# A fused convolution block on one core: the squeeze-and-excite step moved to VectorE, set-up work moved off VectorE, and the seam between the first two stages rebuilt

## The chip, the cores and the metric

The program runs on one core of a Trainium2 chip. The time is the device time of one execution in microseconds. A run gives three executions, and the median of them is the time of the kernel. One further execution was profiled; its instructions are what the views below show.

## The reference, cut to what matters

The input `x` has 16 images of 192 channels and 64x64 pixels, in float32. Two layers follow each other.

```python
# layer 0
h = ln2d(x)                                   # normalise over the 192 channels
projected, gate = split(conv1x1(h, in_proj))  # 192 -> 384
projected = dwconv3(projected, dw_k)
mixed = (four_directional_scans(projected) + dwconv3(projected, le_k)) * sigmoid(gate)
mixed = gelu(batch_norm(mixed))               # statistics over all 16 images
x = x + conv1x1(mixed, out_proj)
x = x + conv1x1(gelu(conv1x1(ln2d(x), fc1)), fc2)   # 192 -> 768 -> 192
# layer 1
pooled = x.mean(axis=(2, 3))                  # one number per image and channel
t = relu(gamma * (pooled @ w1.T - running_mean) * rsqrt(running_var + eps) + beta)   # squeeze, 48 numbers
wt = (t @ w2.T + b2) * mask                   # excite: four 3x3 taps per image and channel are left
out = depthwise_conv(x, wt) + bias
```

## The kernel before, in words

**First stage (0 to 591 us).** The loop `for n in range(n_ac)` runs over 64 chunks of 512 columns, of two images (a pair) each, one in each half of the partitions. For each chunk `turn` (L486, tiles `ps_xt`) transposes pixels on TensorE, `variance` (L493, L494) takes their statistics on VectorE, `project` multiplies by the weights `wi` (L515, tiles `ps_pj`), and the products leave PSUM on VectorE (L520) and ScalarE (L521), into `stg` and `mid` in turn, four chunks to a block. `store` (L539) writes the blocks to DRAM scratch `pg_d`, in five parts by channel group, and `store_first` (L533) sends the first channel group to the tile `low` by DMA. The input tile `xa` has four buffers; `load_a` (L473) asks for it three chunks ahead, half on SyncE's queue and half on GpSimd's.

Work that only sets up the later stages is put between the chunks: `beside(n, f)` in the list `side` calls `f` after chunk `n`. `gate_bias`, `decay_rows`, `projection_bias`, `tap_sums`, `columns`, `sums_across` and `conv_bias` make per-channel biases with small matmuls and small VectorE operations. `vector`, `runs` and `store_vector` build the vectors from which the convolution matrices `dm` and `lm` are read back by `load_dm` (L193) and `load_lm` (L201). `load_weights(k)` loads weights: `k == 1` is the 1.18 MB of `wf1`.

**Second stage (592 to 1265 us).** 96 steps, each with two groups of 64x64 matmuls: `depthwise` (L630, `ps_d`), which uses `dm`, and `local` with `vertical` (L674, `ps_l`), which use `lm`. ScalarE copies `ps_d` into `q` and makes the decay tables `tab` (L653). VectorE runs two scans (L665, L667), the gate (L708) and statistics (L710). A channel group of eight takes four steps; `load_pg` (L617) brings the next group back from DRAM. The seam between the first two stages starts with `hidden_bias` (L141): 36 matmuls with one moving column, put where the first group is on its way to `low`.

**Seam to the third stage (1260 to 1290 us).** `spread` and `batch_norm` turn the statistics into scales through TensorE and VectorE, `keep_up(k)` (L759) issues `k` matmuls that nobody reads, and the first chunk runs without overlap.

**Third stage (1290 to 3557 us).** The loop `for n in range(n_ch + 1)` runs over 64 chunks, eight to a pair. A chunk is one sequence of matmuls: `first` (L997), means and variances, `out_proj` for chunk `n + 2`, and the seven products of `second` (`both`, L852). When a pair has ended (`ended is not None`), `pooled` (L1110) adds up its sums, `squeeze` (L1116) and `excite` (L852, `ps_k`) make the four taps per channel, and `dynamic` spreads the depthwise convolution (L65 and ScalarE) over the next chunks. After the last pair `dynamic_last` runs alone. The order on every engine is the order in which the program is written.

The lines that the steps of the prediction rest on:

```python
for n in range(n_ac):
    if n + 3 < n_ac: load_a(n + 3)
    ...                      # stores of the block before
    project(n, ...); turn(n + 1); deviation(n + 1)
    for f, args in side.pop(n, ()): f(*args)
```

Of the kernel before, what the change touches and what calls it, by code (L numbers as in the profile page):

```python
# [55 lines left out]
def conv_block_kernel(ctx: ExitStack, tc: tile.TileContext, x, prm, w_in, w_out, w_fc1, b_fc1, w_fc2, w1, bn1, w2, out):  # L56
# [46 lines left out]
    w2t = k2.tile([RED, NTAP, C], F32, tag="w2t", name="w2t")  # L103
    b1 = k2.tile([RED, 4], F32, tag="b1", name="b1")
    s1 = k2.tile([RED, 1], F32, tag="s1", name="s1")

    mean64 = k2.tile([128, 64], F32, tag="mean64", name="mean64")

    def load_weights(k):
# [10 lines left out]
        elif k == 3:  # L120
            nc.sync.dma_start(bf1, b_fc1)
            load_cls3(w1t, w1)
            nc.sync.dma_start(w2t, w2[:, 0:NTAP, :])
        else:
            nc.sync.dma_start(b1, bn1)
            nc.sync.dma_start(pv[:, 0], prm[0:128])
            for q in HALF:
                nc.sync.dma_start(pv[q, 1], prm[128:C])


    def squeeze_scale():
# [4 lines left out]
        nc.vector.tensor_scalar_mul(w1t, w1t, 1.0 / NPIX)  # L136

# [28 lines left out]
    ones = ce.tile([128, 128], F32, tag="ones", name="ones")  # L166
    pv = ce.tile([128, 2, NPRM], F32, tag="pv", name="pv")
# [11 lines left out]
    mats[0]["lm"] = lm_even  # L179
    mats[1]["lm"] = mid[:, NPG:NPG + 5 * HW * (GC // 2)].rearrange("p (k m c) -> p k m c", k=5, m=HW)  # L180
# [69 lines left out]
    with ExitStack() as stage:  # L250
# [45 lines left out]
        def gate_bias():  # L296
# [5 lines left out]
            nc.vector.tensor_copy(bias_g, pb[:, 0:C])  # L302

        def by_half(dst, src):

            for i, q in enumerate(HALF):
                nc.vector.tensor_copy(dst[q].rearrange("p (g c) -> p g c", c=GC // 2),
                                      src[q].rearrange("p (g i c) -> p g i c", i=2, c=GC // 2)[:, :, i])
# [23 lines left out]
        def tap_sums(t):  # L332
            taps9 = pt3[lo, t, DW:DW + 9].rearrange("p (i j) -> p j i", j=3)
            for k, rr in enumerate((slice(0, 3), slice(1, 3), slice(0, 2))):
                nc.vector.tensor_reduce(sv[:, t, k, 1:3], taps9[:, 0::2, rr], AX.X, ALU.add)
                nc.vector.tensor_reduce(sv[:, t, k, 0:1], taps9[:, 1:2, rr], AX.X, ALU.add)
                nc.vector.tensor_add(sv[:, t, k, 0:1], sv[:, t, k, 0:1], sv[:, t, k, 1:2])
                nc.vector.tensor_add(sv[:, t, k, 0:1], sv[:, t, k, 0:1], sv[:, t, k, 2:3])
            nc.vector.tensor_scalar_mul(sv[:, t], sv[:, t], bp[:, t:t + 1])
            nc.vector.tensor_scalar_mul(sv[:, t, :, 1:3], sv[:, t, :, 1:3], -1.0)  # L340

        def columns():
            pi = bank()
            nc.tensor.transpose(pi[0:3, 0:128], ind, ident)
            nc.vector.tensor_copy(indt, pi[0:3, 0:128])

        def sums_across(k):
# [3 lines left out]
            nc.vector.tensor_copy(svt, pr[0:3, 0:C])  # L351
# [38 lines left out]
        def vector(k):  # L390
            nc.gpsimd.memset(slots[k % 2], 0.0)
            if k < 3:
                nc.vector.tensor_copy(slots[k % 2].rearrange("g (s c) -> g s c", c=GC)[:, 62:65],
                                      ptg[:, :, DW + 3 * k:DW + 3 * k + 3].rearrange("g c j -> g j c"))
                return
            for i in range(2):
                gv, c = slot(k)[:, i], slice(i * (GC // 2), (i + 1) * (GC // 2))
                if k < 6:
                    le = ptg[:, c, LE + 3 * (k - 3):LE + 3 * (k - 3) + 3]
                    nc.vector.tensor_copy(gv[:, 62:65], le[:, :, ::-1].rearrange("g c j -> g j c"))  # L400
                else:
                    nc.vector.tensor_copy(gv[:, 63:64], gaing[:, c, k - 4:k - 3].rearrange("g c j -> g j c"))

        def runs(i, d):

            gv, c = slot(4)[:, i], slice(i * (GC // 2), (i + 1) * (GC // 2))
            nc.vector.memset(imp, 0.0)
            nc.vector.tensor_copy(imp[:, :, 0:1], gaing[:, c, d:d + 1])
            nc.vector.memset(dcol[:, :, 0:1], 0.0)
            nc.vector.tensor_copy(dcol[:, :, 1:HW], decg[:, c, d:d + 1].broadcast_to([NCG, GC // 2, HW - 1]))  # L410
# [3 lines left out]
            nc.vector.tensor_add(vec, vec, run.rearrange("g c m -> g m c"))  # L414
# [26 lines left out]
        for k, n in enumerate((13, 14, 15, 16, 24, 32, 33, 34)):  # L441
            beside(n, vector, k)
            if k == 4:
                for j in range(4):
                    beside(n + 1 + j, runs, j // 2, j % 2)
            beside(n + (5 if k == 4 else 1), store_vector, k)
        for k in (0, 1, 3, 4):
            beside(40 + k, load_weights, k)
        for i in range(2):
            for h in range(2):  # L450
                beside(45 + 8 * i + 2 * h, load_dm, i, (h,))
                beside(49 + 8 * i + 2 * h, load_lm, i, (h,))
# [82 lines left out]

        def store(blk, d, queues):
# [58 lines left out]
        store_first(blk)  # L595
# [3 lines left out]
    with ExitStack() as stage:  # L599
# [168 lines left out]
        for k in range(-2, n_bp + 1):  # L768
            if 0 <= k + 1 < n_bp:
# [15 lines left out]
            if k == -2:  # L785
                hidden_bias(psb.tile([128, 2, CH], F32, tag="l", name="pb_h")[:, 0])
            if k + 2 < n_bp:
                depthwise(k + 2)
            if 0 <= k < n_bp:
                local(k)  # L790
                sigmoid(k)
            if k in (1, 3, 5):
                scale_hidden(k // 2)
            if k == n_bp - hp_:

# [624 lines left out]
```

## Time and profile before

| | |
|---|---|
| Median of three runs | 3562.65 us (3562.14 to 3562.84) |
| Profiled execution, its own time | 3559.31 us |
| Span of the profiled execution | 3557.5 us |
| Busy share of the span | TensorE 99%, weight loads 53%, VectorE 77%, ScalarE 52%, GpSimd 32% |
| Mean granted TensorE clock | 0.995 |
| Chain that ended last, by engine | TensorE 89%, VectorE 1%, DMA 1% |

A busy share says how long an engine had an instruction in flight. TensorE is one queue: a matmul that is not needed at its place still pushes all that follow it. "Granted clock" is the share of the full TensorE clock in a stretch. Idle time in front of an instruction is shown in brackets with what ended it. The profiled execution was 3.3 us shorter than the median of the runs.

### The profile page before, as it was taken

How to read it: one execution, taken by the hardware profiler on the slowest of the kernel's cores; microseconds unless marked ns; L12 is line 12 of the kernel's file. 1: busy time of each engine (PE TensorE's matmuls, PEld its weight loads, DVE VectorE, ACT ScalarE, POOL GpSimd, SP SyncE). 2: the span in 40 equal slices, each digit the busy share in tenths (PEclk: the TensorE clock that was granted, in tenths of full speed). 3: DMA queues.
4: the chain of work that ended last, by engine and by line, in shares of the span. 5: the costliest groups of instructions: out<-in, count | busy, mean ns of one | idle time of the engine just before them, and what ended most of it. 6: DMA issues, size and time to landing. Idle time of an engine off the chain costs nothing.

```text
span 3557.5 us, 79074 instructions
## 1 busy us (share of the span) xinstructions
PE 3525.5 (99%) x33426; PEld 1874.6 (53%) x33426; DVE 2741.6 (77%) x4722; ACT 1834.7 (52%) x2067; POOL 1155.7 (32%) x1246
## 2 busy tenths in 40 slices
PE   9999999999999999999999999999999999999998
PEld 6666866555555544454444444444445444444443
DVE  7888776999999975557777776777677777767765
ACT  3444445888888844344444445454444444453543
POOL 3434342111111134333333333343433333343433
PEclk9999999999999999999999999999999999999999
DMA  7999998999999941112222222222222222232213
GB/s 177 263 272 264 271 294 282 282 301 283 280 282 286 247 123 34 40 54 60 69 71 70 67 65 81 58 75 62 80 60 69 68 74 62 68 82 58 75 34 90
DMA packets 288987, 492.29 MB, mean 138 GB/s; under 512 B 24816, under 2 KB 183016, under 8 KB 288632
## 3 DMA queue, kind: packets, MB, share of 16 engines
q1 hardware_dynamic: 246772, 341.85, 35.8%
q0 software_dynamic: 40928, 144.36, 14.2%
q8 instruction: 263, 4.31, 0.5%
q10 hardware_dynamic: 932, 1.03, 0.1%
q14 instruction: 92, 0.75, 0.1%
HBM read 284.95 MB, written 197.92 MB: 136 GB/s over the span
## 4 chain that ended last, share of the span: by engine, by line
PE 89%; DVE 1%; DMA 1%; issue 0%; ACT 0%; SPq 0%; ACTq 0%; POOL 0%; DVEq 0%
PE ps_f L997 28%; PE ps_f L852 19%; PE ps_l L674 11%; PE ps_pj L515 7%; PE ps_d L630 7%; PE ps_s L852 7%; PE ps_o L907 5%; PE ps_o L900 2%; PE ps_m L936 1%; PE ps_v L936 1%; PE ps_xt L486 1%; PE ps_k L852 0%; DMA pg_d<-mid 0%; DMA xa<-in_x_dram 0%; DMA mixed_d<-mid 0%
## 5 line engine op out<-in xcount | busy, mean ns | idle before, releaser
L997 PE MATMUL ps_f<-h,wf 64*64 64x512 f32 x9216 | 1014.9, 590 | 0.0
L999 ACT ACTIVATE gl<-ps_f,bf 128x1024 f32<-128x1024 f32 x384 | 427.8, 1114 | 1082.3 <-PE ps_f L997 1080.0
L997 PEld LDWEIGHTS ps_f<-h,wf 64*64 64x64 f32 x9216 | 346.2, 133 | 599.0 <-issue 575.1
L852 PE MATMUL ps_f<-gl,place 128*64 128x256 f32 (+1 forms) x3072 | 528.7, 486 | 1.1 <-ACT rs L979 1.1
L515 PE MATMUL ps_pj<-wi,xa 64*128 64x384 f32 x3072 | 520.1, 488 | 9.2 <-DVE stg L520 6.2
L515 PEld LDWEIGHTS ps_pj<-wi,xa 64*128 64x128 f32 x3072 | 334.0, 189 | 159.9 <-DVE stg L520 10.5
L1032 POOL TENSOR_TENSOR gl<-gl 128x512 f32<-128x512 f32 x192 | 308.6, 1634 | 159.2 <-PE ps_f L852 159.0
L852 PEld LDWEIGHTS ps_f<-gl,place 128*64 128x64 f32 x3072 | 225.2, 137 | 217.7 <-issue 145.8
L1022 POOL COPY turn<-o 128x1 f32<-128x1 f32 x84 | 16.4, 195 | 832.8 <-DVE o L65 832.8
L1028 POOL TENSOR_TENSOR t<-gl 128x512 f32<-128x512 f32 x192 | 246.0, 1281 | 89.0 <-ACT gl L999 44.6
L1030 POOL TENSOR_TENSOR t<-gl,t 128x512 f32<-128x512 f32 x192 | 247.0, 1287 | 44.2 <-ACT gl L999 30.8
L65 DVE SCALAR_TENSOR_TENSOR o<-ximg,taps,o 128x1024 f32<-128x1024 f32 x180 | 231.8, 1288 | 4.9
L473 POOL DMA_DIRECT2D xa<-in_x_dram x192 | 120.2, 634 | 323.8 <-PE ps_pj L515 277.1
L665 DVE TENSOR_TENSOR_SCAN v<-tab,q 128x1024 f32<-128x1024 f32 x96 | 218.3, 2274 | 7.8 <-ACT tab L653 7.8
L667 DVE TENSOR_TENSOR_SCAN v<-tab,q 128x1024 f32<-128x1024 f32 x96 | 217.5, 2266 | 0.0
L1055 DVE SCALAR_TENSOR_TENSOR ximg<-ps_f,pt,ximg 128x256 f32<-128x256 f32 (+1 forms) x176 | 96.6, 549 | 151.2 <-PE ps_f L852 151.2
L653 ACT ACTIVATE tab<-mask,dec_b 128x1024 f32<-128x1024 f32 x192 | 209.6, 1144 | 0.0
L521 ACT ACTIVATE mid<-ps_pj,rsa 128x384 f32<-128x384 f32 x128 | 119.5, 937 | 167.0 <-PE ps_pj L515 150.1
L521 ACT ACTIVATE stg<-ps_pj,rsa 128x384 f32<-128x384 f32 x128 | 119.2, 935 | 162.6 <-PE ps_pj L515 144.2
L913 DVE SCALAR_TENSOR_TENSOR ximg<-ps_o,pt,low 128x256 f32<-128x256 f32 x264 | 113.0, 478 | 93.0 <-PE ps_o L907 90.3
L907 PE MATMUL ps_o<-low,wo 128*64 128x256 f32 x1536 | 182.1, 385 | 0.4 <-ACT low L880 0.4
L493 DVE BATCH_NORM_STATS2 st<-ps_xt 128x6 f32<-128x192 f32 x512 | 171.7, 335 | 8.3 <-PE ps_xt L486 7.7
(258 smaller groups left out, 5604.0 us busy)
## 6 DMA issues: line engine op xcount, KB each, us to landing
low<-in_x_dram SPq DMA_DIRECT2D x128, 384.0 KB
out_dram<-o SPq DMA_DIRECT2D x172, 256.0 KB
mid<-pg_d SPq DMA_DIRECT2D x8, 4096.0 KB
low<-mixed_d SPq DMA_DIRECT2D x116, 256.0 KB
low<-pg_d SPq DMA_DIRECT2D x7, 4096.0 KB
pg_o<-pg_d SPq DMA_DIRECT2D x7, 4096.0 KB
xa<-in_x_dram POOLq DMA_DIRECT2D x192, 128.0 KB, 5.6
xa<-in_x_dram SPq DMA_DIRECT2D x192, 128.0 KB
```

The costliest lines, as they stand in the source:

```text
L65: nc.vector.scalar_tensor_tensor(o, in0, scalar, in1, ALU.mult, ALU.add, **kw)
L515: nc.tensor.matmul(ps[i], pixels(n, t, g)[q], wi[q, t].rearrange("p g k c -> p (g k c)"), start=(t == 0), stop=(t == 2))
L521: nc.scalar.activation(stag[blk][1][:, :, j], ps[1], AF.Copy, scale=rs[:, g, 1:2])
L630: nc.tensor.matmul(dst(ps[o, ih]), mats[g % 2]["dm"][q, di + 1, :, ch], src(s["pg"][q, :, 0, ch]), start=(di == 0), stop=stop)
L674: nc.tensor.matmul(dst(bst[k]["ps"][o, i]), lm_of(g)[q, m, :, c], src(q, ih), start=start, stop=stop)
L852: nc.tensor.matmul(ps[q], w(i), rhs(i), start=start, stop=stop, **kw)
L907: nc.tensor.matmul(ps[wh][q].rearrange("p (r w) -> p r w", w=32), wo[:, 64 * t:64 * t + 64], cols(rows(s["mx"][:, i]))[:, :, wh], start=fi ...
L997: nc.tensor.matmul(pf[o, i], wf1[q, t, m0:m0 + 64], s["h"][q, t], start=(t == 0), stop=(t == 2))
L999: nc.scalar.activation(gl, pf, AF.Gelu, bias=bf1[:, m:m + 1])
L1028: sub(t1[:, m], b12(m), b11(m))
L1030: sub(t2[:, m], b22(m), t1[:, m])
L1032: sub(b12(m), b22(m), b12(m))
```

## The change

1. **Excite on VectorE.** `squeeze` multiplies with the pooled numbers as weights, so that its 48 results stand in every partition. VectorE adds a constant `c0`, multiplies with a table `w2x` of 128x3x4x48 numbers (with the ReLU in the same instruction), sums over the 48, and adds `b2`. The 24 matmuls of `excite` go. The table, the batch norm's scale and the constant are made at the seam to the third stage (`taps_by_channel`, `squeeze_rows`), and `keep_up(4)` there becomes `keep_up(3)`.
2. **First seam.** The last block's first group is copied by VectorE and ScalarE (`keep_first`), not by four DMAs. Three matmuls that nobody reads stand ahead of it. `hidden_bias` moves behind `local(0)`, and the first decay tables are made ahead of the first step.
3. **Set-up work.** PSUM copies of `gate_bias`, `by_half`, `columns` and `sums_across` go from VectorE to ScalarE. Small operations of `tap_sums`, `vector` and `runs` go to GpSimd; the part of `runs` that fills its inputs becomes `ready`, a chunk earlier. VectorE keeps the reductions and the scan.
4. **Loads.** `load_dm` and `load_lm` of group 0 are issued at chunks 46, 50, 54 and 58; those of group 1 at 60 and 61; `wf1` at 62. `w2t` is loaded late in the second stage, into the space of a `dm` tile.

```diff
+    def squeeze_rows(pr):
+        nc.tensor.matmul(pr[:, 0:2 * RED], ones[0:RED], sq_d.rearrange("p k r -> p (k r)"), start=True, stop=True)
+        nc.vector.tensor_mul(w1t, w1t, pr[:, 0:RED].unsqueeze(1).broadcast_to([128, 3, RED]))
+        nc.vector.tensor_copy(c0, pr[:, RED:2 * RED])
+    def taps_by_channel(pk):
+        for t in range(3):
+            for k in range(NTAP):
+                j = (2 * t + k % 2) * RED
+                for q in HALF:
+                    nc.tensor.matmul(pk[q, k // 2, j:j + RED], w2t[:, k, 64 * t:64 * t + 64], ident[0:RED, 0:RED],
+                                     start=True, stop=True)
+        for h in range(2):
+            nc.scalar.activation(w2x[:, :, 2 * h:2 * h + 2], pk[:, h, 0:6 * RED].rearrange(...), AF.Copy)
...
-                nc.vector.tensor_add(sv[:, t, k, 0:1], sv[:, t, k, 0:1], sv[:, t, k, 1:2])
+                nc.gpsimd.tensor_add(sv[:, t, k, 0:1], sv[:, t, k, 0:1], sv[:, t, k, 1:2])
...
+        def ready(i, d):
+            c = slice(i * (GC // 2), (i + 1) * (GC // 2))
+            nc.gpsimd.memset(imp, 0.0)
+            nc.gpsimd.tensor_copy(imp[:, :, 0:1], gaing[:, c, d:d + 1])
+            nc.gpsimd.memset(dcol[:, :, 0:1], 0.0)
+            nc.gpsimd.tensor_copy(dcol[:, :, 1:HW], decg[:, c, d:d + 1].broadcast_to([NCG, GC // 2, HW - 1]))
         def runs(i, d):
...
             nc.vector.tensor_tensor_scan(flat(run), flat(dcol), flat(imp), 0.0, ALU.mult, ALU.add)
-            nc.vector.tensor_add(vec, vec, run.rearrange("g c m -> g m c"))
+            nc.gpsimd.tensor_add(vec, vec, run.rearrange("g c m -> g m c"))
...
-        for k in (0, 1, 3, 4):
+        for k in (0, 3, 4):
             beside(40 + k, load_weights, k)
-        for i in range(2):
-            for h in range(2):
-                beside(45 + 8 * i + 2 * h, load_dm, i, (h,))
-                beside(49 + 8 * i + 2 * h, load_lm, i, (h,))
+        for h in range(2):
+            beside(46 + 4 * h, load_dm, 0, (h,))
+            beside(54 + 4 * h, load_lm, 0, (h,))
+        beside(60, load_dm, 1)
+        beside(61, load_lm, 1)
+        beside(62, load_weights, 1)
...
-        store_first(blk)
+        warm_ = bank()
+        for _ in range(3):
+            nc.tensor.matmul(warm_[:, 0:2 * C], ident, wi[:, 0].rearrange("p g k c -> p (g k c)"), start=True, stop=True)
+        keep_first(blk)
...
-            if k == -2:
-                hidden_bias(psb.tile([128, 2, CH], F32, tag="l", name="pb_h")[:, 0])
             if k + 2 < n_bp:
                 depthwise(k + 2)
             if 0 <= k < n_bp:
                 local(k)
                 sigmoid(k)
+            if k == 0:
+                hidden_bias(psb.tile([128, 2, CH], F32, tag="d", name="pb_h", bufs=2)[:, 0])
...
-        keep_up(4)
+        taps_by_channel(psb.tile([128, 2, CH], F32, tag="d", name="pk_h", bufs=2))
+        keep_up(3)
...
         batch_norm()
+        squeeze_rows(psb.tile([128, 2, CH], F32, tag="d", name="pr_h", bufs=2)[:, 0])
...
         for t in range(3):
-            nc.tensor.matmul(pt[0:RED, 0:2], w1t[:, t], pool2[:, t], start=(t == 0), stop=(t == 2))
+            for i, q in enumerate(HALF):
+                nc.tensor.matmul(pt[q, 0:RED], pool2[q, t, i:i + 1].broadcast_to([64, 64]), w1t[q, t], start=(t == 0), stop=(t == 2))
...
+        nc.vector.tensor_add(red, pt[:, 0:RED], c0)
+        nc.vector.scalar_tensor_tensor(flat(prod), red.unsqueeze(1).broadcast_to([128, 3 * NTAP, RED]), 0.0, flat(w2x), ALU.max, ALU.mult)
+        nc.vector.tensor_reduce(taps.rearrange("p t k -> p (t k)"), flat(prod), AX.X, ALU.add)
+        nc.vector.tensor_add(taps, taps, pt3[:, :, B2:B2 + NTAP])
-    def excite(p):
-        pk = ps2.tile([128, 3, NTAP, 1], F32, tag="a", name="ps_k")
-        for t in range(3):
-            for k in range(NTAP):
-                both(pk[:, t, k], lambda i: w2t[:, k, 64 * t:64 * t + 64], lambda i: s["red"][:, i:i + 1], True, True)
-        nc.vector.tensor_add(taps, pk[:, :, :, 0], pt3[:, :, B2:B2 + NTAP])
```

## The prediction

> **What bounds the kernel now.** The page comes first, then TensorE's waits, the windows, the chain of waits, and the timeline at the places that the change touches. The page (busy time, share, instructions):
>
> ```profile
> PE 3525.5 (99%) x33426; PEld 1874.6 (53%) x33426; DVE 2741.6 (77%) x4722; ACT 1834.7 (52%) x2067; POOL 1155.7 (32%) x1246
> ```
>
> TensorE is in flight for all but 32 us, so only two things can shorten the span: fewer or faster matmuls, and fewer TensorE waits. The waits (total us, times, longest):
>
> ```profile
> PE ps_xt L486 <- DMA xa<-in_x_dram: 6.3, 3, 3.1
> PE ps_pj L515 <- DVE stg L520: 6.2, 6, 2.0
> PE ps_pj L515 <- DVE mid L520: 2.5, 3, 1.3
> PE pb_h L141 <- ACT mid L521: 1.1, 1, 1.1
> ```
>
> Nearly all of the waiting is in the first stage, on input tiles and on evictions. The windows say what follows a wait (columns: stretch; busy PE, PEld, DVE, ACT, POOL; granted clock; DMA share; GB/s):
>
> ```profile
> 290.00:400.00 110.00, 110.00 (x910) 90.39 (x908) 90.57 (x278) 48.48 (x65) 48.62 (x84) 1.00 0.97 272
> 411.00:418.00 7.00, 5.54 (x38) 3.73 (x40) 0.98 (x4) 0.00 (x0) 3.62 (x7) 0.52 1.08 312
> 585.00:590.00 5.00, 5.00 (x34) 3.05 (x32) 2.52 (x3) 2.56 (x3) 0.00 (x0) 1.00 0.00 0
> 597.00:599.00 2.00, 2.00 (x13) 0.79 (x17) 0.16 (x1) 0.00 (x0) 0.00 (x0) 0.50 1.00 325
> ```
>
> From 290 to 400 us no time is lost: the first transposes of successive chunks are 8.54 us apart, and VectorE is busy 90.57 of 110 us, 7.0 us per chunk, which leaves it 1.5. DMA is at 0.97, so extra transfers there cost time. After the wait at 412 us, and after `hidden_bias` at 592, the clock is at half: an input wait is paid twice. From 585 to 590 the DMA engines do nothing.
>
> Three steps of the chain (start, us, what), and two rows of the timeline inside the second chunk, show a pair boundary:
>
> ```profile
> 1533.89 5.31 PE ps_f L997 x48
> 1568.62 5.31 PE ps_f L997 x48
> 1605.25 5.31 PE ps_f L997 x48
> ```
>
> ```profile
> 1593.19 1.56 PE L852 MATMUL ps_k<-red,w2t 48*64 48x1 f32 x48
> 1590.74 0.48 DVE L1055 SCALAR_TENSOR_TENSOR spare<-ps_f,pt,spare 128x256 f32<-128x256 f32 x1 [2.48 <-PE ps_f L852]
> ```
>
> A chunk takes 34.73 us, a chunk that ends a pair 36.63. The premium of 1.90 comes seven times: 1.49 for `excite` (1593.19 to the next product at 1594.68) and 0.41 for `squeeze`. The eighth pair ends in the tail.
>
> **First stage, set-up work: +6.2 us.** Chunk starts in the timeline give the loss. With `tap_sums`, 99.39 to 126.84 is 27.45 for three chunks, where 25.63 is normal: 1.8. With `runs`, 249.84 to 288.94 is 39.10 for four, where 34.17 is normal: 4.9. Each `tap_sums` puts 1.8 us between VectorE's statistics (100.50 to 102.32), of which the six reductions, under 0.9, stay. Each `runs` puts in 2.3 (251.45 to 253.70), of which the scan of 0.68 stays. Both remainders fit into 1.5, so I take 6.2 of 6.7; with half of `tap_sums` left and some waiting for GpSimd's input, 5.0. `conv_bias` (1.06 lost at each of three chunks), `gate_bias` and `decay_rows` (1.3 each) lose time on TensorE and in the rotation of PSUM banks; an eviction by ScalarE instead of VectorE changes neither, so nothing is counted (0 to 1).
>
> On GpSimd the new operations stand ahead of the next chunk's `load_a` half and its two stores, and wait for VectorE at the chunk's end, perhaps 3 us. What hides that: GpSimd's `xa` lands 5.6 us after its issue and is needed two chunks, 17 us, later, so 11.5 us are free.
>
> **First stage, loads: +10.5 us.** Three places lose time: 400.45 to 433.40 takes 32.95 for three chunks (7.3 lost, including the half clock), 450.49 to 461.41 loses 2.4, and 521.19 to 532.04 loses 2.3, 12.0 in all. In front of the first, SyncE's queue issues `wo`, `wf1` and small weights between the `xa` loads. Moving `wf1` (1.18 MB) and group 1's matrices (1.44 MB) takes 2.62 of 4.3 MB out of a stretch where DMA has no room, and spreads group 0's 1.44 MB over 13 chunks. `wo`'s loads (7 us of SyncE's issue time) and the small ones stay; I leave 1.5 lost, and 6 if half of the stalls come back. The 2.62 MB are issued at 60 to 62, where no `xa` load follows: at 285 GB/s they take 9.2 us, and 581 to 592 is empty. `wf1` is first needed near 604, group 1's `dm` near 617. SyncE's last stores and `load_pg(1)` stand behind them; if that hole did not cover them, the first step of group 1 would be late by at most those 9.2 us. On SyncE and GpSimd the four transfers of `store_first` go.
>
> **First seam: +0.3 us (-1 to +2.5).** Before, the last projection ends at 591.2, `pb_h` fills 592.30 to 597.02, and the fourth `depthwise` starts at 611.85. After: two copies on VectorE and two on ScalarE of 64x256 after the last eviction at 592.2, at some 0.4 each (ScalarE's 128x256 of L979 took 0.42), so `depthwise(0)` starts near 593.2. The three idle matmuls (6 passes of 384 columns at 0.32, 1.9 us) end before that. Then three `depthwise` of 2.6 (6.89 a step less 4.28 for `ps_l`), `local(0)` 2.6, `hidden_bias` 4.0 (36 at the 0.112 spacing that most had), `vertical(0)` 1.7: 609.3, a gain of 2.5. `hidden_bias` is not free at its new place, since TensorE has no idle time in this stage; VectorE's `bf1` sum waits behind `scans(1)` for it, with the gate queued behind, but the gate needs `vertical(0)`, later still. The clock then decides. In the row TensorE was in flight from 592.30 on, and the clock still halved from 595.7 to 602.5, costing 3.4 us. Four microseconds of one-column matmuls in a new place should do so again for one or two spells of 3.4: 1.7 to 3.4 lost. I take 2.2.
>
> The Trainium skill ("TensorE: Matmul & The Clock Gate", Part 1) ties the half clock to an idle window of about 3.4 us in a free-running grid. Read strictly, a gapless `hidden_bias` would leave the clock alone and the seam would gain 2.5; the row speaks against that reading.
>
> **Seam to the third stage: -1.1 us (-3 to -0.3).** The chain here is gate, statistics (end 1264.87), `pm` at 1264.93; TensorE's four `keep_up` (3.43) end just before. Three of them take 2.57, and `taps_by_channel` adds 48 passes. Lower bound: `ps_k`'s 48 in 1.56. Upper: 67 ns each (18 of `projection_bias` in 1.21), 3.2. The nearest in columns are the transposes (24 of 64 columns in 0.91), so 1.8. That puts `pm` 0.7 to 1 us late. `squeeze_rows` puts two VectorE operations (0.3 and 0.2) ahead of a transpose that ScalarE needs little later. ScalarE's two copies of `w2x` sit in a wait of 9.75. A half-clock spell stands at 1271.5 already; a second would cost 1.7.
>
> **Pair boundaries: +9.7 us.** `excite`'s 1.49 goes. The new `squeeze` has 12 passes: 0.39 at `ps_k`'s 33 ns, 0.81 at 67 ns; by the transposes 0.46 against 0.41 before. Seven times 1.49 less 0.05 is 10.1; the upper bound gives 7.6; I take 9.7. On VectorE 0.66 (0.27, 0.22, 0.17) goes and a chain comes ahead of the residuals: add 0.2, multiply 576 near 0.75 (L1055's 512 took 0.74), reduction 0.65, add 0.17: 1.8. The 1.1 us more lie in the 2.48 us that VectorE waits at 1590.74. If that cover were gone, each boundary would lose 1.1. The next in line is `ps_s` at 1597.32, now due near 1595.8: it waits for the L1055 behind the residuals, done near 1595.1.
>
> **Tail: +0.5 us (0 to 0.9).** From `pooled` (3520.28) to the taps (3523.31) is 3.03; with 0.45 for `squeeze` and the 1.8 chain, and crossings, near 2.5.
>
> **Sum.** 6.2 + 10.5 + 0.3 - 1.1 + 9.7 + 0.5 = 26.1. The profiled 3559.31 becomes 3533.2; it was 3.3 below the median, so the median 3562.65 becomes 3536.5. All low ends together give 14.6 (3548), all high ends 32.5 (3530).
>
> **Rivals.** *The first stage stays full.* DMA at 0.97 to 1.0 leaves no room for the earlier chunks either, and the stalls move to other chunks: for it speaks the DMA row, against it the 110 us without loss. Loads and half of the set-up gain go: 12 us left, 3550. *The excite moves the wait.* VectorE's chain reaches past its idle 2.48 and TensorE waits at `ps_s`: 8 to 10 us go, 3545; against it the margins above. *GpSimd's queue holds up the input (slower).* `ready`, `runs` and `tap_sums` wait for VectorE with `load_a` behind them. If they hold it for over 11.5 us, a chunk loses what 400 to 433 lost, 7.3. Five of the chunks with such work would cost 36 and give 3573; two or three would cancel most of the gain. Against it: VectorE trails TensorE by some 2 us.
>
> **How the numbers follow.** The forecast has 0.77, the full first stage 0.10, the moved wait 0.09, the queue 0.04. The likeliest sum is 3536.5. With the ends above and a little beyond for the clock, 3528 to 3550. What can be told from no change here is 0.2%, 7 us. Faster 0.93, the same 0.04, slower 0.03.
>
> **What would show it.** Right: chunks 8.54 apart where `runs` and the loads stood, no half clock near 411, the 585 to 590 window full of DMA, `depthwise(0)` near 593, a half-clock spell after `pb_h`, `pm` later after the gate, and 35.2 at pair boundaries. Wrong: TensorE waits on `xa` in the first 400 us, on group 1's tiles near 617, or on VectorE at `ps_s`.

## The result, and the profile after

The changed kernel took 3541.52 us (median of 4 runs, 3539.46 to 3543.24) beside 3562.74 us for the kernel before (4 runs, 3562.14 to 3568.18): a ratio of 0.9936, with a 95% interval of 0.9920 to 0.9952. That is 21.2 us less. The forecast was 26.1 us less (3536.5, range 3528 to 3550). The profiled execution after took 3541.40 us with a span of 3539.6, so 17.9 us of span are to be accounted for against the profiled 3557.5 of before. The other 3.3 of the 21.2 us lie in no row below: the profiled execution of before was 3.4 us under its median, that of the changed kernel 0.1.

First the page's busy times of the changed kernel, then its longest TensorE waits (total us, times, longest).

```profile
PE 3512.9 (99%) x33144; PEld 1919.0 (54%) x33144; DVE 2741.6 (77%) x4666; ACT 1839.7 (52%) x2086; POOL 1171.1 (33%) x1302
```

```profile
PE ps_pj L547 <- DVE stg L552: 6.8, 2, 5.3
PE ps_d L1212 <- issue: 2.5, 1, 2.5
PE ps_xt L518 <- DMA xa<-in_x_dram: 2.1, 1, 2.1
PE ps_i L1259 <- DVE c L146: 1.4, 1, 1.4
```

The waits on input tiles fell from 6.3 us to 2.1, and what is left of them stands at the very start. The waits on evictions into `stg` did not go. There were six with 6.2 us together; now there are two with 6.8, one of them 5.3 long. The last row is new: the idle matmuls of the third stage wait for VectorE's copy `c0`. VectorE and ScalarE are as busy as before.

The windows of the changed kernel (stretch; busy PE, PEld, DVE, ACT, POOL; granted clock; DMA share; GB/s):

```profile
290.00:400.00 110.00, 108.48 (x919) 90.94 (x917) 87.87 (x264) 47.61 (x64) 50.46 (x90) 1.00 0.95 279
411.00:418.00 7.00, 7.00 (x66) 6.94 (x64) 5.71 (x19) 2.94 (x5) 2.97 (x5) 1.00 0.94 264
447.00:451.00 4.00, 3.42 (x12) 2.00 (x14) 2.87 (x10) 1.21 (x2) 0.00 (x0) 0.58 0.93 259
585.00:590.00 5.00, 5.00 (x81) 4.32 (x79) 1.88 (x1) 2.53 (x5) 0.00 (x0) 1.00 1.00 326
598.00:604.00 6.00, 6.00 (x32) 2.37 (x36) 1.59 (x3) 1.92 (x2) 0.00 (x0) 0.50 1.02 416
```

The half clock near 411 is gone, and another has appeared at 447. The stretch from 290 to 400, which lost nothing before, now loses 1.5 us, although its DMA share is no higher. From 585 to 590 the DMA engines are full; the last projection now ends at 581.0, where it ended at 591.2. After `hidden_bias` the clock is at half, as it was.

A pair boundary in the changed kernel: steps of the chain (start, us, what), then VectorE's new chain in the timeline, from the sum that waits for `squeeze` to the taps, and its next wait.

```profile
1527.13 5.31 PE ps_f L1046 x48
...
1561.86 5.31 PE ps_f L1046 x48
...
1579.63 0.33 PE ps_t L1166 x12
...
1596.92 5.31 PE ps_f L1046 x48
```

```profile
1580.00 0.21 DVE L1168 TENSOR_TENSOR red<-ps_t,c 128x48 f32<-128x48 f32 x1 [4.40 <-PE ps_t L1166]
1580.24 0.87 DVE L1171 SCALAR_TENSOR_TENSOR prod<-red,w2x 128x576 f32<-128x576 f32 x1
1581.14 0.75 DVE L1173 TENSOR_REDUCE taps<-prod 128x12 f32<-128x576 f32 x1
1581.93 0.17 DVE L1174 TENSOR_TENSOR taps<-taps,pt 128x12 f32<-128x12 f32 x1
...
1584.05 0.49 DVE L1104 SCALAR_TENSOR_TENSOR spare<-ps_f,pt,spare 128x256 f32<-128x256 f32 x1 [1.06 <-PE ps_f L901]
```

A chunk takes 34.73 us, and one that ends a pair 35.06. The premium is the 0.33 of `squeeze` and nothing else. The VectorE chain takes 2.1 us (1580.00 to 1582.10). Behind it VectorE still waits 1.06 at its next product, where it waited 2.48 before: the cover was there, and 1.4 of it is used.

Where the 17.9 us went, from the chunk starts and the rows at the seams of both traces (minus is less time):

| place | forecast | measured |
|---|---|---|
| start of the kernel | none | -0.9 |
| chunks with `tap_sums` and `runs` | -6.2 | -6.6 |
| chunk ahead of 309 us | none | +1.8 |
| loads: 400 to 433 us of before | | -7.35 |
| loads: the chunk that ended at 461 us before, 453 after | | +5.0 |
| loads: the chunk that ended at 532 us before, 522 after | | -2.0 |
| loads together | -10.5 | -4.3 |
| first seam, last projection to `depthwise(4)` | -0.3 | +1.8 |
| seam to the third stage | +1.1 | +1.7 |
| seven pair boundaries | -9.7 | -11.0 |
| tail | -0.5 | -0.1 |

The rows add up to 17.6 us; 0.3 lies in none of them. `depthwise` is counted from 0: `depthwise(4)`, which the expectations below call the fourth, is the first behind all half clock. The prediction's fourth, at 611.85, is `depthwise(3)`; it came 0.6 later, with part of the half clock still ahead.

The body of the second stage takes 642.66 us in both. Three things stand against the forecast: 6.8 us that came back in the first stage (1.8 and 5.0), the first seam, and the boundaries, which brought more than reckoned. The experiments take the parts by themselves and then these three.

### The profile page after: what moved, and what is told of

Same layout as the page of the kernel before. It is cut to its first block, busy times and chain, and to the rows that moved or that the text cites. A ratio compares the mean times of both kernels' runs of the same rounds, so it can differ in the third digit from the quotient of the medians.

```text
span 3539.6 us, 78530 instructions
## 1 busy us (share of the span) xinstructions
PE 3512.9 (99%) x33144; PEld 1919.0 (54%) x33144; DVE 2741.6 (77%) x4666; ACT 1839.7 (52%) x2086; POOL 1171.1 (33%) x1302
## 2 busy tenths in 40 slices
DMA packets 288745, 492.00 MB, mean 139 GB/s; under 512 B 24752, under 2 KB 182824, under 8 KB 288392
## 3 DMA queue, kind: packets, MB, share of 16 engines
q0 software_dynamic: 40912, 144.37, 14.2%
## 4 chain that ended last, share of the span: by engine, by line
PE 98%; DMA 1%; DVE 1%; issue 0%; ACT 0%; POOL 0%; SPq 0%; ACTq 0%; DVEq 0%
PE ps_f L1046 28%; PE ps_f L901 19%; PE ps_pj L547 14%; PE ps_l L718 12%; PE ps_d L674 7%; PE ps_s L901 7%; PE ps_o L956 5%; PE ps_o L949 2%; PE ps_xt L518 1%; PE ps_m L985 1%; PE ps_v L985 1%; DMA xa<-in_x_dram 0%; DVE ol L65 0%; PE ps_i L1259 0%; DVE o L65 0%
```

## The experiments

Each time stands beside the median of the kernel before on the same chip, taken in the same session: 3561.19 for the first four, 3561.7 for the next four, 3561.89 for the three after, and 3562.49 for the last. "Less than before" below is the difference from these.

**The parts alone.** Two theories on the first stage went in. *Place*: TensorE waits only where a load stands on a queue ahead of something that is needed next. *Volume*: the DMA engines have no room, and what TensorE saves comes back as waits. Each of the four parts was put into the kernel before by itself.

e1, `excite` and `squeeze` alone:

```diff
+        taps_by_channel(psb.tile([128, 2, CH], F32, tag="d", name="pk_h", bufs=2))
-        keep_up(4)
+        keep_up(3)
...
-            nc.sync.dma_start(w2t, w2[:, 0:NTAP, :])
...
-            excite(ended)
```

> The kernel before with only the excite and squeeze of the change (the taps' sums on VectorE, w2x and c0 prepared at the end of the second stage, w2's load late in that stage). If the parts add up: the chunk that ends a pair 35.06 us where it was 36.63, seven times, 11.0 us; the seam to the third stage 1.7 us longer, the tail within 0.3: 9.0 to 9.6 us less in all. If the seam's loss came from the other parts of the change (a later start, another clock phase): 10.5 to 11 us less.

Measured: 3548.15 (5 runs), ratio 0.9964 (0.9951 to 0.9977), 13.0 us less, more than either expectation. Boundaries and the seam to the third stage came as expected (-11.0 and +1.9 in the trace). Some 3 us of the trace come from the first stage, which this part was thought not to touch. It takes `w2`'s 147 kB off SyncE's queue there, and the waits between 340 and 530 us shrank. That the bytes are the reason is not shown, since the kernel before and e4 differ by as much with one and the same first stage (table below). The profiled run gave it back in the first seam, by a wait that is shown below.

e2, the set-up work alone:

```diff
-                nc.vector.tensor_add(sv[:, t, k, 0:1], sv[:, t, k, 0:1], sv[:, t, k, 1:2])
+                nc.gpsimd.tensor_add(sv[:, t, k, 0:1], sv[:, t, k, 0:1], sv[:, t, k, 1:2])
...
+                    beside(n + j, ready, j // 2, j % 2)
                     beside(n + 1 + j, runs, j // 2, j % 2)
```

> The kernel before with only the set-up work of the first stage moved to GpSimd and ScalarE. Both theories: the chunks with tap_sums and runs fall to 8.54 to 8.75 us, 6.6 us less. Theory 'volume' (the DMA engines have no room, what TensorE saves comes back as waits on DMA): the waits near 300 us and from 400 us on grow by most of that, 0 to 3 us less in all. Theory 'place' (a wait comes only where a load stands on a queue ahead of what is needed next): the later waits stay as they were, apart from the 1.8 us seen near 309 us in the changed kernel, 4.5 to 6.6 us less in all.

Measured: 3556.72 (10 runs), ratio 0.9987 (0.9978 to 0.9997), 4.5 us less. In the trace the chunks with `tap_sums` and `runs` give 6.2 us. The three chunks that took 32.95 at 400 to 433 us then take 36.4, so half of the saving is given back there; 1.2 more is near 309 and 348 us, and 2.2 is regained behind. That lies between the two theories, and the interval (1.1 to 7.8 us less) takes in both.

e3, the loads alone:

```diff
-        for k in (0, 1, 3, 4):
+        for k in (0, 3, 4):
             beside(40 + k, load_weights, k)
-        for i in range(2):
-            for h in range(2):
-                beside(45 + 8 * i + 2 * h, load_dm, i, (h,))
-                beside(49 + 8 * i + 2 * h, load_lm, i, (h,))
+        for h in range(2):
+            beside(46 + 4 * h, load_dm, 0, (h,))
+            beside(54 + 4 * h, load_lm, 0, (h,))
+        beside(60, load_dm, 1)
+        beside(61, load_lm, 1)
+        beside(62, load_weights, 1)
```

> The kernel before with only the loads moved (wf1 and group 1's matrices to the last chunks, group 0's matrices over chunks 46 to 58). tap_sums and runs still slow TensorE by 6.6 us before the loads come. Both theories: the waits of 400 to 433 us (7.3) and near 525 us (2.3) go. Theory 'volume': the DMA engines had 6.6 us more time before, so the 7.4 us stall at the first eviction of the block at chunk 48 is gone or under 2: 10 to 12 us less in all. Theory 'place': that stall stays at 5 to 7.5 us, since the order on SyncE's queue is the same: 3 to 6 us less in all.

Measured: 3560.15 (10 runs), ratio 0.9994 (0.9985 to 1.0004), 1.0 us less, so no difference that can be told: less than either theory expected. The 400 to 433 stretch fell from 32.95 to 26.6, but the later chunk rose from 10.92 to 15.99, as in the changed kernel, and the one near 530 stayed at 10.5. That the stall stays is what *place* expected: it does not depend on the time that TensorE loses before 290 us. A reason that would fit *volume* too is that `xa` has only four buffers, so that DMA cannot run far ahead; this was argued, not tried. The part to which the forecast gave 10.5 us is worth about 1 us alone. The profiled execution (3552.43) was the fastest of the ten and 6.9 us shorter than that of before, but only 1.7 of this lies in the stretch with the loads; 3.0 lies ahead of 26 us, and it shows no half clock in the seam to the third stage.

e4, the first seam alone:

```diff
-        store_first(blk)
+        warm_ = bank()
...
+        keep_first(blk)
...
-            if k == -2:
-                hidden_bias(psb.tile([128, 2, CH], F32, tag="l", name="pb_h")[:, 0])
+            if k == 0:
+                hidden_bias(psb.tile([128, 2, CH], F32, tag="d", name="pb_h", bufs=2)[:, 0])
```

> The kernel before with only the first seam changed (the copies instead of store_first at the end, the idle matmuls, hidden_bias after local(0)). If the clock is what eats the gain: the last projection to the fourth depthwise takes about 29.3 us where it took 27.5, two half-clock spells after hidden_bias, 1.5 to 2.1 us more in all. If in the changed kernel it was the loads in the last chunks that delayed the seam: 1.5 to 3 us less in all.

Measured: 3562.07 (10 runs), ratio 1.0001 (0.9992 to 1.0011), 0.9 us more. From the last projection to the fourth `depthwise` it takes 29.28 us where it took 27.53, with every load where it was before. In the trace the seam part loses by itself, as the first theory had it; the time does not show it (2.8 us less to 3.9 more). The four differences add up to 17.6 us, the whole gave 21.2.

**What fills the first stage.** The stall of the changed kernel, on TensorE and VectorE, and SyncE's queue ahead of it (timeline rows of the changed kernel; in brackets the wait and what ended it):

```profile
447.58 5.83 PE L547 MATMUL ps_pj<-wi,xa 64*128 64x384 f32 x24 [5.30 <-DVE stg L552]
```

```profile
446.61 0.92 DVE L552 TENSOR_SCALAR stg<-ps_pj,rsa 128x384 f32<-128x384 f32 x1 [6.80 <-DMA pg_d<-mid]
```

```profile
434.51 1.84 SPq L218 DMA_DIRECT2D dm<-dv_d  x1
436.53 2.27 SPq L505 DMA_DIRECT2D xa<-in_x_dram  x3
438.84 1.25 SPq L580 DMA_DIRECT2D pg_d<-stg  x2
...
443.13 2.53 SPq L565 DMA_DIRECT2D low<-mid  x2
```

The first eviction of a block waits until the last stores out of the same buffer have landed. Those two stores (438.84) were issued behind group 0's `dm` (434.51). VectorE's row names a store out of `mid`; that those out of `stg` end the wait is read from the program, since the trace has no landing of theirs. It fits both theories. e5 put the four loads behind the last stores of a block:

```diff
-            beside(46 + 4 * h, load_dm, 0, (h,))
-            beside(54 + 4 * h, load_lm, 0, (h,))
+            beside(47 + 4 * h, load_dm, 0, (h,))
+            beside(55 + 4 * h, load_lm, 0, (h,))
```

> The changed kernel with group 0's four loads one chunk later: after the last stores of a block (chunks 47, 51, 55, 59) instead of before them (46, 50, 54, 58). Theory 'place': the 5.3 us wait on VectorE's eviction into stg near 447 us falls under 1 us and the half clock after it goes; chunk 48 takes 8.5 to 9 us where it took 15.96; 6 to 7.4 us less than the changed kernel in all. Theory 'volume': the same bytes in the same 13 chunks find no room either; 4 to 7 us of waits appear at other chunks between 440 and 580 us, and the time stays within 3 us of the changed kernel.

Measured: 3540.33 (5 runs), ratio 0.9939 (0.9926 to 0.9951), the time of the changed kernel. The wait at 447 fell from 5.3 to 3.3 us, and no half clock followed (the chunk took 12.80 instead of 15.96). 1.9 us came at other chunks, before and after. Place may have a share in this stall, but the time does not show it.

e6 took bytes away instead. The four transfers by which each block copies group 0's part from SBUF to SBUF became ScalarE copies, one per chunk:

```diff
-                    store_first(blk - 1)
                     store(blk - 1, 0, (nc.gpsimd, nc.sync))
                 store(blk - 1, part + 1, (nc.gpsimd, nc.sync))
+                keep_part(blk - 1, part)
```

> The changed kernel with store_first's transfers (262 kB per block, 2.8% of what a block moves) replaced by ScalarE copies in every block, one per chunk. Theory 'volume': the DMA engines get 2.8% more room in the whole stage, 0.9 us per block, 2.6 us by 309 us and 10 us by the end, so both the 1.8 us near 309 us and most of the 7.4 us near 447 us go; 6 to 9 us less than the changed kernel. Theory 'place': the 1.8 us may go, the stall near 447 us stays at 5 us or more, because the load still stands ahead of the last stores; 0 to 4 us less.

Measured: 3531.61 (5 runs), ratio 0.9921 (0.9909 to 0.9933), 30.1 us less than before, 8.9 more than the change brought. The two windows with the stalls, in this kernel:

```profile
300.00:320.00 20.00, 20.00 (x176) 12.79 (x174) 16.14 (x49) 9.80 (x16) 12.93 (x24) 1.00 0.94 260
440.00:452.00 12.00, 12.00 (x97) 9.24 (x95) 10.10 (x32) 5.68 (x9) 3.64 (x7) 1.00 1.00 285
```

TensorE is busy throughout, and every chunk near 309, 447 and 520 us takes 8.54. `dm` stands where it stood ahead of the last stores. The bytes that the page counts fell from 492.00 to 488.05 MB. At 285 GB/s the 262 kB of a block are 0.92 us, an estimate from the second row; that was enough. The time is at the upper end of what *volume* expected.

Bytes are not all that went. The share of the DMA engines from 60 to 290 us fell by more than 2.8% (the changed kernel, then this one):

```profile
60.00:290.00 230.00, 229.73 (x1934) 149.62 (x1931) 187.25 (x576) 101.98 (x145) 108.24 (x212) 1.00 0.94 268
60.00:290.00 230.00, 229.74 (x1932) 149.32 (x1930) 187.36 (x577) 111.69 (x172) 101.67 (x200) 1.00 0.87 262
```

The four transfers also leave the queues: in the changed kernel SyncE issues from 425.03 to 449.52 with gaps under 0.2 us, and its part of `store_first` (443.13, above) takes 2.53 of that.

e9 kept those bytes and changed their order only:

```diff
                 if part == 0:
-                    store_first(blk - 1)
                     store(blk - 1, 0, (nc.gpsimd, nc.sync))
+                if part == 2:
+                    store_first(blk - 1)
```

> The changed kernel with store_first's four transfers of each block at the block's third chunk instead of its first: the same bytes, another order. Theory 'volume': the two stalls of the first stage (near 309 and 447 us, 9.2 us together) stay, 7 to 11 us together, though they may stand at other chunks; the time within 3 us of the changed kernel. Theory 'order' (store_first stood ahead of the stores that release stg): the stalls go as they did with ScalarE's copies, 6 to 9 us less than the changed kernel.

Measured: 3541.31 (6 runs), ratio 0.9938 (0.9926 to 0.9950), again the changed kernel's time. The chunk ahead of 309 takes 8.54, but 0.9 us are lost near 342, 5.9 near 445 and 2.2 near 520.

All kernels side by side: what the chunks from 290 us to the end of the stage took over 8.54 us each, summed from the chunk starts.

| kernel | us over 8.54 per chunk |
|---|---|
| before; e4 (same first stage) | 12.5; 15.4 |
| e2, set-up alone | 15.0 |
| e3, loads alone | 10.8 |
| e1, excite alone (no `w2` load) | 9.3 |
| after; e7 and e8 (same first stage) | 9.9; 11.0 and 7.5 |
| e5, loads one chunk later | 8.6 |
| e9, `store_first` later | 9.3 |
| e10, before with ScalarE's copies | 8.0 |
| e6, after with ScalarE's copies | 0.0 |
| e11, e12 (with ScalarE's copies) | 0.4, 0.2 |

Kernels with the same first stage differ by 3 us, so neither order (e5, e9) is told apart from the changed kernel. The transfers themselves are: without those of `store_first`, 2.8% of the bytes, nearly all of it went, in three kernels. The first stage of the changed kernel has run into what its DMA takes. Whether the bytes, the time of the DMA engines or the time to issue decides was not tried apart.

e10 asked whether that also holds before the change, with ScalarE's copies as the only edit:

```diff
-                    store_first(blk - 1)
                     store(blk - 1, 0, (nc.gpsimd, nc.sync))
                 store(blk - 1, part + 1, (nc.gpsimd, nc.sync))
+                keep_part(blk - 1, part)
```

> The kernel before with nothing of the change, and store_first's transfers in the blocks but the last replaced by ScalarE copies, one per chunk. Theory 'volume': the 2.8% of room that the DMA engines get takes most of the waits of 400 to 433 us (7.3) and those near 455 and 525 us (2.4 and 2.3) away although every load stands where it stood, 8 to 11 us less than before. Theory 'place': wf1 and wo still stand between the input tiles on SyncE's queue, so the 7.3 us stay at 5 or more; 2 to 5 us less than before.

Measured: 3555.53 (8 runs), ratio 0.9979 (0.9969 to 0.9989), 6.4 us less, between the two expectations. The later stalls shrank by 3.0 us, but 400 to 433 still takes 31.95, as *place* had it, with a wait on an eviction into `mid` in place of the one on input (timeline row of this kernel):

```profile
418.20 5.88 PE L515 MATMUL ps_pj<-wi,xa 64*128 64x384 f32 x23 [3.04 <-DVE mid L520]
```

A burst as large as `wf1` with `wo` and the small weights is not covered by 0.9 us per block. Whether its bytes or its place on SyncE's queue does it was not tried apart. Either way the change was right to take `wf1` from there (26.6 in e3).

**The first seam.** Four rows of TensorE in the changed kernel's timeline, then two of the kernel before:

```profile
594.19 4.59 PE L163 MATMUL pb_h<-pt,wf 64*128 64x1 f32 x36
598.71 3.70 PE L718 MATMUL ps_l<-v,low 64*64 64x512 f32 x16
602.19 3.99 PE L674 MATMUL ps_d<-low,dm 64*64 64x512 f32 x40
...
610.29 2.79 PE L674 MATMUL ps_d<-pg_o,dm 64*64 64x512 f32 x40
```

```profile
592.30 4.79 PE L141 MATMUL pb_h<-pt,wf 64*128 64x1 f32 x36 [1.10 <-ACT mid L521]
...
618.73 2.78 PE L630 MATMUL ps_d<-pg_o,dm 64*64 64x512 f32 x40
```

There is no gap around `hidden_bias` in the changed kernel. `vertical(0)` takes 3.5 us where 1.7 is normal, and `depthwise(3)` 3.8 where 2.6 is. `depthwise(4)` starts 29.3 us after the last projection (580.97); before it was 27.5 (after 591.20).

The order of the seam does not set how many spells of half clock, of 3.4 us each, follow `hidden_bias`. With the old order there was one in e1 and e3, two in before and e10, three in e2 and e12 (a window of each below); with the new one, one in e6 and e9, two in the changed kernel, e4, e5 and e8.

```profile
590.00:600.20 10.20, 10.20 (x61) 7.78 (x64) 0.16 (x1) 0.00 (x0) 3.17 (x6) 0.50 0.95 301
573.60:583.80 10.20, 10.20 (x69) 7.39 (x72) 0.16 (x1) 0.00 (x0) 2.71 (x5) 0.50 0.95 306
```

At two spells the old order has `depthwise(4)` after 27.5 us (before, e10) and the new one after 29.3 (all four kernels), so the new order itself costs 1.8. A spell costs nearly as much: the old order takes 29.2 at three, the new one 27.5 and 27.9 at one. e7 cut `hidden_bias` into three:

```diff
-            if k == 0:
-                hidden_bias(psb.tile([128, 2, CH], F32, tag="d", name="pb_h", bufs=2)[:, 0])
-            if k in (1, 3, 5):
-                scale_hidden(k // 2)
+            if k in (0, 1, 2):
+                hidden_bias(psb.tile([128, 2, CH], F32, tag="d", name="pb_h", bufs=2)[:, 0], range(2 * k, 2 * k + 2))
+            if k in (3, 5, 7):
+                scale_hidden((k - 3) // 2)
```

> The changed kernel with hidden_bias in three pieces of two columns (12 narrow matmuls, about 1.5 us each) after local(0), local(1) and local(2), and scale_hidden two steps later each. Theory 'narrow matmuls in one stretch': the clock stays full, since pieces of 1.5 us like the old excite's never halved it; last projection to fourth depthwise 26 to 27.5 us where it is 29.3; 2 to 3.4 us less than the changed kernel. Rival 'the seam': the half clock comes from the gap and the switch between stages and stays with or without the pieces; within 0.5 us of 29.3.

Measured: 3541.68 (6 runs), ratio 0.9950 (0.9938 to 0.9962), not faster than the changed kernel. A window after the first piece and a later row of its timeline:

```profile
597.00:605.00 8.00, 8.00 (x92) 4.87 (x91) 7.38 (x7) 7.59 (x9) 0.64 (x1) 1.00 1.05 389
```

```profile
639.63 2.91 PE L675 MATMUL ps_d<-mid,dm 64*64 64x512 f32 x40 [1.69 <-DMA dm<-dv_d]
```

The clock stays full. The expectation named `depthwise(4)`, which comes 25.0 us after the last projection, earlier than expected, since a third of `hidden_bias` still lies behind it. `depthwise(6)`, behind all three pieces, starts after 40.44 us instead of 43.10: 2.7 us gained, within the 2 to 3.4 expected. Then TensorE waits 1.69 for group 2's `dm`. At `depthwise(8)` the gain is 0.8 (56.09 against 56.89). The half clock had been covering a DMA wait. Runs with one spell ahead instead of two show the same: e1, with the old order, waits for group 1's tile (timeline row of e1), and e3 waits 1.5, e9 2.0.

```profile
615.24 4.45 PE L655 MATMUL ps_d<-pg_o,dm 64*64 64x512 f32 x40 [2.78 <-DMA pg_o<-pg_d]
```

**The seam to the third stage.** In the changed kernel, TensorE and then VectorE:

```profile
1261.92 0.46 PE L144 MATMUL pr_h<-sq_d,ones 48*128 48x96 f32 x2
1263.80 3.44 PE L1259 MATMUL ps_i<-wf,ident 128*128 128x512 f32 x4 [1.43 <-DVE c L146]
```

```profile
1263.45 0.20 DVE L146 COPY c<-pr_h 128x48 f32<-128x48 f32 x1
```

`c0`'s copy is the last reader of the second stage's PSUM, it stands behind batch norm's chain on VectorE, and the third stage's first idle matmuls need that PSUM. e8:

```diff
+            if k == 8:
+                squeeze_rows(psb.tile([128, 2, CH], F32, tag="d", name="pr_h", bufs=2)[:, 0])
...
-        keep_up(3)
+        keep_up(2)
...
-        squeeze_rows(psb.tile([128, 2, CH], F32, tag="d", name="pr_h", bufs=2)[:, 0])
```

> The changed kernel with squeeze_rows moved to the eighth step of the second stage and keep_up(3) cut to keep_up(2) in the seam. Theory 'the idle matmuls wait for c0's copy': the first idle matmul of the third stage no longer waits 1.4 us on VectorE, out_proj starts 2 to 2.6 us earlier after the last vertical, the seam falls from 31.0 to 28.5 to 29.8 us. Rival 'the seam is set by ScalarE's normalisation chain behind': out_proj starts earlier but the third stage's first chunk does not, seam within 0.4 us of 31.0.

Measured: 3540.97 (5 runs), ratio 0.9942 (0.9930 to 0.9954); a gain this small cannot be told by the times. In the trace the idle matmuls wait 0.27 instead of 1.43, and `out_proj` starts 12.6 us after the last `vertical` instead of 14.2, less than the 2 to 2.6 expected. 0.4 of it is there at `pm` already, by the shorter `keep_up`. The seam takes 29.4 where it took 31.0, so it is not set by ScalarE's chain.

**Together.** e11 has e6, e7 and e8 in the changed kernel, and both halves of group 2's `dm` on GpSimd's queue:

```diff
-            (nc.sync, nc.gpsimd)[i].dma_start(mats[g % 2]["dm"][q].rearrange("p k m c -> p k (m c)"), src)
+            (nc.gpsimd if g == 2 else nc.sync, nc.gpsimd)[i].dma_start(mats[g % 2]["dm"][q].rearrange("p k m c -> p k (m c)"), src)
```

> The changed kernel with ScalarE's copies in every block, hidden_bias in three pieces, squeeze_rows early with keep_up(2), and both halves of group 2's dm on GpSimd's queue. If the gains stand each by itself: first stage without the 9.2 us of stalls, no half clock in the first seam and no 1.7 us wait on group 2's dm (last projection to the sixth depthwise after it 40.4 us or less, where it was 43.1), seam to the third stage 1.7 us shorter: 12 to 14 us less than the changed kernel. If the wait on dm comes from the DMA engines being full there, and not from SyncE's queue, about 1.7 us of that is lost again.

Measured: 3526.40 (4 runs), ratio 0.9898 (0.9885 to 0.9910): 35.5 us less than before, 14.3 more than the change brought. It is the fastest kernel of this study, and the gains stood side by side. Its waits have

```profile
PE ps_d L674 <- DMA mid<-pg_d: 2.1, 1, 2.1
```

With `dm` early, group 2's pixels (`mid<-pg_d`) are next late: `depthwise(8)` comes 56.31 us after the last projection. Another queue for one of two late transfers did not help here, where the DMA share is 0.98 (573 to 627 us). e12 put the old seam into e11:

```diff
-        keep_first(blk)
+        store_first(blk)
...
+            if k == -2:
+                hidden_bias(psb.tile([128, 2, CH], F32, tag="l", name="pb_h")[:, 0])
```

> The kernel of the run before (e11) with the first seam as it was before the change: store_first's transfers at the end of the first stage, no idle matmuls, hidden_bias in one piece in the gap ahead of depthwise(0), dm of group 2 on both queues. ScalarE's copies in the other blocks, the early squeeze_rows and the rest of the change stay. Theory 'the seam part loses': from the last projection to depthwise(8) the old order takes 55.1 us with two half-clock spells, as in the kernel before, where e11 took 56.3; 1 to 1.5 us less than e11. Rival 'the DMA engines set it': TensorE then waits for a tile of group 1 or 2 and depthwise(8) comes 56 us or more after the last projection; within 0.5 us of e11 or slower.

Measured: 3529.77 (4 runs), ratio 0.9910 (0.9893 to 0.9926). Neither mechanism: no wait for a tile, but three half-clock spells (573.6 to 583.8 us, the second window above) instead of two, and 56.75 us to `depthwise(8)`. Since the old order shows one, two or three spells, the third is as far as known chance, and the expectation, which took two for granted, stays untested. The old and the new seam cannot be told apart by the time (the intervals overlap).

## Why the prediction was right, and where its steps were not

The forecast of a clear gain and the range held. The order of the terms did not: the loads, forecast as the largest, came third. The total missed by 5 us, and that it missed by so little is partly luck: the profiled executions differ by 17.9 us, 8 less than forecast, with errors in both directions among the terms. The high ends of the terms, with none of the loads' 12.0 us left over, add up to 31.9, or to 32.9 with the 1 us of `conv_bias`, not to 32.5; nothing hangs on it.

**Pair boundaries, 9.7: 11.0.** Right, and above the upper end of 10.1. The term took the new `squeeze` for 0.05 us dearer than the old one. Its 12 passes took 0.33 us, 28 ns each, less than the 0.41 before. VectorE's chain was reckoned at 1.8 and took 2.1; the cover was there, and TensorE does not wait at `ps_s`.

**Set-up work, 6.2: 6.6.** Right by place and by size, and in e2 too. `conv_bias`, `gate_bias` and `decay_rows` lose what they lost. What the step left out is what a faster TensorE asks of DMA: 1.8 us came back ahead of 309 us (1.0 and 0.3 in e7 and e8, which have the same first stage), and half of the saving in e2.

**Loads, 10.5: 4.3, and 1.0 alone (e3).** This is the mis-sized term; 4.3 lies under its own low end of 6. The step said that DMA at 0.97 had no room, and then treated group 0's matrices, spread over 13 chunks, as if they had some, leaving 1.5 us lost. Behind the first of them a longer stall came, which cost 5.0 us with its half clock. The rival "the first stage stays full" had the right mechanism and got 0.10, but its 3550 was too slow. Measured, 6.8 us of the first stage's gain came back, and e6 against e9 shows that the transfers of `store_first` were too many, and not their order wrong. The argument against the rival, 110 us without a loss, was weak: that stretch held hardly a load of weights (`wo` and the first of `wf1` at its end) and was at 0.97 all the same, so it left 0.03 for the loads to come. The Trainium skill ("DMA: Bandwidth & Descriptors", Bandwidth) gives about 358 GB/s per core as the limit for transfers between HBM and SBUF, and says that this is a core's share when both cores of a pair stream. By that figure, an estimate, the 279 GB/s of this stretch would leave a fifth. The runs differ: without 2.8% of the bytes, 9.9 us of loss were gone.

**First seam, +0.3: -1.8.** Below the low end of -1. The sum set a new order at full clock (with 2.2 off for the clock) against a measured old order that itself held 3.4 us of half clock. Both traces have two spells, 6.8 us of half clock each, so the clock cancels. What remains is that `hidden_bias` filled a gap of 5.8 us before and now lies on TensorE's path with 4.5, while the gap shrank by 3.6; and 0.9 is spread over the first steps. A third point was not seen: what is next late. In the five kernels in which TensorE came earlier or had fewer spells (e1, e3, e7, e9, e11) it waited 1.5 to 2.8 us for a tile of group 1 or 2, and `depthwise(8)` started 55.1 to 58.1 us after the last projection in every kernel profiled. Only e6, with fewer bytes, had one spell and no wait. The Trainium skill ("TensorE: Matmul & The Clock Gate", Part 1) has the clock fall after an idle window of about 3.4 us. In all twelve kernels with the 36 one-column matmuls in one piece it fell during or behind them, though the records show no idle time among them; with 12 at a time (e7, e11) it did not. By the old order 1.1 us without a matmul stood ahead of them, by the new one none. Why one, two or three spells follow stays open.

**Seam to the third stage, -1.1: -1.7.** Within its range. `pm` was 0.6 late, reckoned at 0.7 to 1. The two VectorE operations of `squeeze_rows` were counted for the transposes behind them, not for the PSUM that they hold; e8 gives that back.

**Tail, 0.5: 0.1.** The taps are ready 0.4 earlier, and the end hardly moves: `ps_d` waits 2.5 us on "issue".

**The other rivals.** TensorE never waits at `ps_s`. GpSimd's queue held up no input: after the start no wait on `xa` is left.

## What to carry to other kernels

Here a stage without a TensorE wait and with DMA at 0.95 to 1.0 was balanced, not free: 3.5 of the 6.2 us that e2 took off TensorE came back as one longer stall, and transfers of 2.8% of the bytes decided about 9 us. Before moving loads within such a stage, look for bytes that an idle engine can carry, here a copy inside SBUF that ScalarE did beside its work. Compare a new order with the old one at the same clock, here at the same number of spells, and before counting a clock loss as a gain to be had, ask which transfer arrives next.

## What the runs showed of the hardware

- 36 matmuls of 64x1 without a gap among them (4.2 us at full clock in e6 and e9) were followed or overtaken by half clock in one to three spells of 3.4 us in all twelve kernels that had them in one piece. The first spell began between 1.0 us (e2) and 5.3 us (e9) after the first of them. In pieces of 12 matmuls (1.5 us) with wide matmuls between them, no spell came (e7, e11).
- In the first stage a DMA share of 0.94 to 1.00 moved 260 to 285 GB/s in the windows shown (e6, after). In the first seam a share of 1.02 to 1.05 moved 389 to 416 (e7, after).
- A ScalarE copy of a 64x256 block per chunk, 6.5 us more ScalarE time in the 110 us from 290 to 400, took the place of 2.8% of the DMA bytes and delayed no eviction that TensorE waited for.
